# A two-layer graph network on one core: the last quad by one level of the short product, its graphs normalised alone, the first degrees planned with a longer transfer, and a new order of the work

## The chip, the core and the metric

The kernel runs on one core of a Trainium2 chip. A core has five engines with a program each: TensorE (PE, matmuls, with a separate load of the stationary operand, PEld), VectorE (DVE), ScalarE (ACT), GpSimd (POOL) and SyncE (SP, which only issues transfers here). Matmuls write to eight PSUM banks of 128 partitions by 512 numbers. The metric is the device time of one execution in microseconds (us); less is better. Everything is computed in 32-bit floating point.

## What is computed

There are 128 graphs of 128 nodes with 512 features each. `x` and `adj` are the inputs, `W`, `W1`, `W2`, `W3` the weights.

```python
def layer0(x, adj, W):
    deg = jnp.sum(adj, axis=-1, keepdims=True)
    agg = jnp.einsum('bij,bjf->bif', adj, x) / jnp.maximum(deg, 1e-6)
    return relu(jnp.einsum('bnf,of->bno', jnp.concatenate([x, agg], 2), W))

def gcn(x, adj, W, b):
    return jnp.einsum('bnm,bmh->bnh', adj, jnp.einsum('bnf,fh->bnh', x, W)) + b

def layer1(x, adj):
    x = relu(gcn(x, adj, W1, b1))
    x = relu(gcn(x, adj, W2, b2))
    return gcn(x, adj, W3, b3)

x = layernorm(x + layer0(x, adj, W))
x = layernorm(x + layer1(x, adj))
```

## The kernel before

**Quads.** Four graphs make a quad, 512 rows; there are 32 quads (`NG`). Each of the big products of a quad (512 rows by 512 features by 512 columns) is done in a short form of block multiplication: the matrices are cut in two by two blocks, sums and differences of blocks are made, and seven block products stand for eight. The products carry numbers 1 to 7, with 1 and 5 first, and results are put together from them by copies on ScalarE (L570 into an SBUF tile `s`, L576 into another bank, L636 and L806 into the result) and adds on VectorE (L325).

- With **one level**, `product` (L590) is one block product: four matmuls of 128x256.
- With **two levels**, each of the seven is cut again in the same way: `inner_product` (L608) works on 128x128 blocks, 49 matmuls of 128x128 in place of 28 of 128x256. The sums of the second level are made by `inner_sums`, for the data on GpSimd into tiles `ti`, in part over the data themselves, and for W2 and W3 once, on VectorE: they overwrite the block `b01` of each weight form by `b01 - b00`. The function `two(q)` says that W2 and W3 are multiplied by two levels for all quads but the first. The layer-0 product does so from quad 2 on, with the forms of W0 (there called "forms") kept in DRAM and streamed through `ring` and `big` tiles.

**Stages.** Each quad passes the stages X (load of the transposed x and its sums), D (adjacency and degrees), AT (transposed adjacency), L0 to L3 (layer-0 product), A0 and A1 (aggregation with the normalised adjacency, first layernorm), G0 to G3 (aggregation for layer 1, L897), Ha and Hb (product with W1), Sa and Sb (product with W2), H2 (aggregation with relu, L978 and L989), Ta and Tb (product with W3), and Z0 and Z1 (aggregation of two graphs each, L1018, residual, second layernorm, output). The products with W1 are always of one level; bias and relu follow on ScalarE (L942).

**Order.** The whole program is written out at build time. A string `ORDER` lists stages with a lag ("Tb-5" is stage Tb of the quad five behind), `AFTER` says which stages a stage has to follow, and a planner (`Plan`) takes the resulting list of operations, estimates a cost for each, works out a latest time for each, and fills the five engines' programs by a simulation of its own. Constants steer it: `HELP` (how near its latest time an add of GpSimd has to be for VectorE to take it), `HOLD` (how long a bank may stay full), `LEADS` (how much ahead of its latest time an operation may start: for the seeding of banks, a second use, the data's inner sums, and the streamed forms). Each engine then runs its program strictly in order. Only SP and, for quad 0's degrees, ScalarE issue transfers; these rotate over eight completion semaphores, and a transfer waits for the one before it on its semaphore.

**The degrees.** `degrees(q)` (L546 to L548) sums the rows of the four adjacencies, takes the larger of sum and 1e-6, and its reciprocal, `deg`. It writes these 512 numbers to DRAM (`dd`), and reads them back as one row that is repeated over all partitions (`ah`), to scale the transposed adjacency. The second transfer waits for the first. For quad 0 both are on ScalarE's queue. The planner counts the first with a size of 400,000 bytes; it moves 2 KB.

**The end.** The last quad (31) does the same as the others: two-level S and T stages with inner sums on GpSimd or VectorE, then Z0 and Z1, each with two graphs' layernorm: VectorE's statistics (L821, L822), a square root on ScalarE (L826), reciprocal and a multiply on VectorE (L829, L833), the two graphs' scaling on ScalarE (L841), and their outputs of 256 KB each by SP. By `AFTER`, Z0 and Z1 both follow Tb.

Of the kernel before, what the change touches and what calls it, by code (L numbers as in the profile page):

```python
# [14 lines left out]
P = 128  # L15
# [20 lines left out]
class Plan:  # L36
# [5 lines left out]


    LAG = 0.15
    AHEAD, HELP, HOLD, SEEN, REST, SPARE = 32, 12.0, 3.0, 8, 15.0, 1
    DMA_US, DMA_RATE = 2.0, 0.22e6

    def __init__(self, pools):
# [176 lines left out]

BANKS = 8
SIZES = 8, 3, 7, 6
LEADS = 3.8, 7.0, 45.3, 276.2
AFTER = {
    "X": "L2-1+1 L3-1+1", "D": "A0-1 A1-1 D-1", "AT": "Z0-2 Z1-2", "L0": "X D AT A1-1 A0-1 Z0-2 Z1-2", "L1": "L0", "L2": "L1", "L3": "L1 L2<2",  # L230
    "A0": "L2 L3", "A1": "L2 L3", "G0": "A0 Hb-1", "G1": "A0 Hb-1", "G2": "A1 Hb-1", "G3": "G0 G1 G2 A1",
    "Ha": "G3 Tb-1!", "Hb": "Ha", "Sa": "Hb Z0-1! Z1-1!", "Sb": "Sa", "H2": "Sb", "Ta": "H2", "Tb": "Ta", "Z0": "Tb", "Z1": "Tb",
}
ORDER = """
    Tb-5 Tb-5 AT-4 L0-4 Sa-5 D L1-4 H2-5 L1-4 L1-4 L2-4 L3-4 L2-4 L2-4 L3-4 L2-4 L1-4 H2-5 Sb-4 Z1-6 H2-5 A1-4 A1-4
    H2-5 Z1-6 G0-4 H2-5 L0-3 Z0-6 Ha-4 Sb-4 Ha-4 A0-4 L3-4 X-3 D L2-4 Sb-4 L0-3 Hb-4 Tb-5 Tb-5 G1-4 L0-3 Ta-5 G2-4
    G1-4 L2-4 Tb-5 G3-4 L2-4 L3-3 L2-4 Ta-5 Ta-5 G0-4 Ta-5 Ha-4 Ta-5 A1-4 A0-4 G3-4 Z0-5 L0-3 Ta-5 AT-3 Hb-4 L0-3 G2-4
    L1-3 Sa-4 L0-3 Sb-4 Ta-5 Sa-4 Ta-5 L3-3 Hb-4 Tb-5 Sa-4 Sb-4 Ha-4 X-2 Sb-4 Sa-4 Sa-4 L1-3 A0-3 Z1-5 Z0-5 L3-3 Sb-4
    Sb-4 L3-3 L1-3 Sa-4 Ha-3 Ha-3 Sa-4 L0-3 L1-3 Tb-4 Tb-4 L3-3
"""  # L240


# [1 line left out]
def gnn_resnorm_kernel(  # L244
# [62 lines left out]
    def pinned(ins):  # L307
        return tc.keep_in_program_order(ins)
# [11 lines left out]
    def const(v):  # L320
        return lambda: v
# [14 lines left out]
    class Weight:  # L336
# [17 lines left out]
        def inner_sums(self, over=()):  # L354
            for ps in HALVES:
# [5 lines left out]
                for dst, a, b, reads, writes in (  # L361
# [4 lines left out]
                ):  # L366
                    add("DVE", len(ps) * P, const(dst), const(a), const(b), reads, writes, OP.subtract, True)

        def to_forms(self, s):

            for ps in PAIRS:
                n = len(ps)
                t = self.t[:, ps[0] : ps[-1] + 1].rearrange("p k c (o n) -> p k c o n", o=2)
                b00, b01, b10, b11 = (t[:, :, c, o] for c in range(2) for o in range(2))
                raw = [(self.name, p) for p in ps]
                f, e = Slot("ti"), Slot("ti")

                def form(sl, j, n=n):
                    return lambda: TI_T[sl.index][:, j, 0:n]

                def send(i, src, reads, ps=ps):
                    dma(
                        const(FORMS[i - 1][:, ps[0] : ps[-1] + 1, s]), src, reads, [("form", s, i, p) for p in ps],
                        len(ps) * P * P * 4,
                    )

                def sub(dst, a, b, reads, writes, n=n):
                    add("DVE", n * P, dst, a, b, reads, writes, OP.subtract, True)

                sub(form(f, 1), const(b11), const(b01), raw, [f, e, (f, 1)])  # L390
                sub(form(f, 0), const(b01), const(b00), raw, [f, (f, 0)])
                sub(form(e, 0), const(b11), form(f, 0), raw + [f, (f, 0)], [e, (e, 0)])
                sub(form(e, 1), const(b10), form(e, 0), raw + [e, (e, 0)], [e, (e, 1)])
                send(1, const(b00), raw)
                send(2, const(b10), raw)
                send(3, const(b11), raw)
                send(7, form(f, 1), [f, (f, 1)])
                send(5, form(f, 0), [f, (f, 0)])
                send(6, form(e, 0), [e, (e, 0)])
                send(4, form(e, 1), [e, (e, 1)])  # L400
# [25 lines left out]
    class Data:  # L426
# [8 lines left out]
        def keys(self, places, cs=range(2), gs=range(2)):  # L435
            return [(self.name, p, c, g) for p in places for c in cs for g in gs]

        def sums(self):
            for d, a, b, op in ((3, 1, 5, OP.add), (2, 3, 0, OP.subtract), (1, 0, 1, OP.subtract), (6, 4, 2, OP.subtract)):
                add(  # L440
                    "POOL", F, const(self.t[:, d]), const(self.t[:, a]), const(self.t[:, b]),
                    self.keys((a, b)), self.keys((d,)), op,
                )

        def inner_sums(self):
# [96 lines left out]
    def degrees(q):  # L542
# [3 lines left out]
        vector(512, lambda: pinned(nc.vector.tensor_reduce(d, AR_T, axis=AX.X, op=OP.add)), ["ar"], kd)  # L546
        vector(90, lambda: pinned(nc.vector.tensor_scalar(d, d, DEG_EPS, None, op0=OP.max)), kd, kd, True)
        vector(90, lambda: pinned(nc.vector.reciprocal(d, d)), kd, kd)  # L548
        dma(const(dd.rearrange("g i -> i g")), const(d), kd, [("dd", q % 2)], 400000, queue)
        dma(  # L550
            const(AH_T), const(bass.AP(tensor=dd.tensor, offset=dd.offset, ap=[[0, P], [P, G], [1, P]])),
            [("dd", q % 2)], ["ah", "row of degrees"], 400000, queue,
# [258 lines left out]
    def rows_b(key, a, b, t):  # L811
        yield from wino_b(key, a, b, copy_to(t, 1, 0), sums_to(t, 0, 1))

    def layernorm(i, ap, keys):

        i %= ND
        mv, rs = MV_T[i], RS_T[i]
        for j in range(2):
            st = ST_T[(2 * i + j) % ND]
            ks = [("st", (2 * i + j) % ND)]  # L820
            vector(512, lambda j=j, st=st: pinned(nc.vector.bn_stats(st, ap(j))), keys(j), ks)  # L821
            vector(98, lambda j=j, st=st: pinned(nc.vector.bn_aggr(mv[:, j, :], st)), ks, [("mv", i, j)])  # L822
        mk = [("mv", i, 0), ("mv", i, 1)]
        kr, kb = ("rs", i, 1), ("rs", i, 2)
        scalar(
            2, lambda: pinned(nc.scalar.activation(rs[:, 0, :], mv[:, :, 1], AF.Sqrt, bias=EPS_T)), mk + ["eps"], [kr],  # L826
            columns=1,
        )
        vector(90, lambda: pinned(nc.vector.reciprocal(rs[:, 0, :], rs[:, 0, :])), [kr], [kr])  # L829
        vector(  # L830
            90,
            lambda: pinned(
                nc.vector.scalar_tensor_tensor(rs[:, 1, :], mv[:, :, 0], -1.0, rs[:, 0, :], op0=OP.mult, op1=OP.mult)  # L833
            ),
            mk + [kr], [kb], True,
        )
        for j in range(2):
            scalar(
                512,
                lambda j=j: pinned(  # L840
                    nc.scalar.activation(ap(j), ap(j), AF.Identity, bias=rs[:, 1, j : j + 1], scale=rs[:, 0, j : j + 1])  # L841
                ),
                [kr, kb] + keys(j), keys(j), columns=2,
            )

    WBA = Streamed()
# [108 lines left out]
    def seg_h1_b(q):  # L955
        d = data(q, "h1")
        yield from wino_b(("h1", q), data(q, "g1"), W1, lambda p: relu_to(d, 1, p), sums_h1(q, 0, 1), transposed=True)
        d.sums()
        if two(q):
            d.inner_sums()  # L960

    def seg_s2_a(q):
        yield from (single_a if two(q) else rows_a)(("s2", q), data(q, "h1"), W2, row(q, "s2"))

    def seg_s2_b(q):
        yield from (single_b if two(q) else rows_b)(("s2", q), data(q, "h1"), W2, row(q, "s2"))

    def seg_h2(q):
        d, s = data(q, "h2"), row(q, "s2")
        a, ka = at(q)  # L970
        for o in (2, 3, 0, 1):
# [22 lines left out]
                [p, "b2"], d.keys((4 * h, 4 * h + 1), (c,)), columns=1,  # L994
            )
            yield
        d.sums()
        if two(q):
            d.inner_sums()

    def seg_s3_a(q):
        yield from (single_a if two(q) else rows_a)(("s3", q), data(q, "h2"), W3, row(q, "s3"))

    def seg_s3_b(q):
        yield from (single_b if two(q) else rows_b)(("s3", q), data(q, "h2"), W3, row(q, "s3"))

    def seg_last(q, m):
# [3 lines left out]
        for j, o in enumerate(os):  # L1011
# [11 lines left out]
                "DVE", F, lambda o=o: S_T[o.index], lambda p=p: bank_ap(p), const(u.graph(g)),  # L1023
                [p] + u.keys((g,)), [o],
            )
            yield
        layernorm(4 * q + 2 + m, lambda j: S_T[os[j].index], lambda j: [os[j]])
        for j, o in enumerate(os):
            dma(
# [157 lines left out]
```

## Time and profile before

The median of three runs is 2274.39 us, from 2273.63 to 2274.56. The profiled execution took 2272.34 us; its span from the first to the last instruction is 2270.6 us at a mean granted TensorE clock of 0.997.

| engine | busy us | share of the span | instructions |
|---|---|---|---|
| PE | 2241.7 | 99% | 13704 |
| PEld | 1973.0 | 87% | 13704 |
| DVE | 1555.7 | 69% | 3321 |
| POOL | 1274.7 | 56% | 1673 |
| ACT | 1236.9 | 54% | 2378 |

PE's first matmul starts at 8.54 us, its last ends at 2261.18. The costliest groups of PE are the two-level products (L608), then the one-level ones (L590), then the aggregations (L872, L897, L978, L1018). Some unit times of the trace, which serve as measures: four matmuls of 128x256 take 1.73 us, one of 128x128 takes 0.2225, one of 128x512 takes 0.86; ScalarE copies 128x512 in 0.59, VectorE adds 128x512 in 0.69, GpSimd in 1.27.

How to read the rows that follow in the next section: the list of waits tells which engine and line waited for which other, for how long in total, how often and how long at most. A row of windows gives a stretch of the span, its length, each engine's busy time in it, the granted clock of PE as a share of full speed, the share of time that the transfer engines were busy, and GB/s. The chain of waits goes back from the last instruction to what released it; each row is a start, a length and what was done; "q" behind an engine's name (SPq, ACTq) is its queue issuing a transfer. A tile is named without its number.

### The profile page before, as it was taken

To read this page: it belongs to the slowest core of one execution; us is meant where nothing else is said; L and a number is where in the kernel's file an instruction comes from. 1 tells how busy PE (TensorE), PEld (TensorE's weight loads), DVE (VectorE), ACT (ScalarE), POOL (GpSimd) and SP (SyncE) were. 2 spreads that over 40 slices of the span, in tenths; PEclk is the share of its full clock that TensorE was granted. 3 is DMA by queue.
4 is the path that set the end of the run, shared out by engine and by line. 5 is a ranking of instruction groups with operands and counts; after the bars stand their busy time and mean duration, and the time that the engine had idled before them with its cause. 6 is when DMAs were issued, how large, how long until landed. Compare 5 with 4: busy or idle time off the path is not lost.

```text
span 2270.6 us, 39980 instructions
## 1 busy us (share of the span) xinstructions
PE 2241.7 (99%) x13704; PEld 1973.0 (87%) x13704; DVE 1555.7 (69%) x3321; ACT 1236.9 (54%) x2378; POOL 1274.7 (56%) x1673
## 2 busy tenths in 40 slices
PE   8999999999999999999999999999999999999997
PEld 6888888898898888888988988888888888898895
DVE  4766667766676667677666776676776667666666
ACT  2455555555555555555555555555555555555554
POOL 0236655656656566556565565665565655656641
PEclk9999999999999999999999999999999999999999
DMA  7644445534455444555344554445553445534431
GB/s 232 156 144 132 137 157 167 178 116 148 132 174 170 136 139 131 161 171 166 125 140 138 179 170 128 143 133 161 170 157 125 137 146 170 174 116 143 126 103 38
DMA packets 218330, 333.14 MB, mean 147 GB/s; under 512 B 39313, under 2 KB 83857, under 8 KB 218129
## 3 DMA queue, kind: packets, MB, share of 16 engines
q1 hardware_dynamic: 217456, 330.33, 46.1%
q8 instruction: 110, 1.80, 0.4%
q14 instruction: 92, 0.75, 0.1%
q10 hardware_dynamic: 672, 0.26, 0.0%
HBM read 290.46 MB, written 40.04 MB: 146 GB/s over the span
## 4 chain that ended last, share of the span: by engine, by line
PE 97%; DMA 1%; DVE 1%; ACT 0%; issue 0%; POOL 0%; SPq 0%; ACTq 0%; DVEq 0%
PE bank L608 58%; PE bank L590 20%; PE bank L897 5%; PE bank L978 5%; PE bank L1018 5%; PE bank L872 5%; DMA dd<-deg 0%; DMA s<-in_x_dram 0%; DMA big<-in_w0T_dram 0%; ACT s L570 0%; ACT s L841 0%; DVE st L821 0%; DVE T L325 0%; POOL ti L327 0%; DVE xT L325 0%
## 5 line engine op out<-in xcount | busy, mean ns | idle before, releaser
L570 ACT COPY s<-bank 128x384 f32<-128x384 f32 (+1 forms) x569 | 307.7, 541 | 512.7 <-PE bank L608 340.5
L590 PE MATMUL bank<-T,w 128*128 128x256 f32 x1792 | 407.2, 379 | 0.0
L590 PEld LDWEIGHTS bank<-T,w 128*128 128x128 f32 x1792 | 335.7, 190 | 43.9 <-issue 0.5
L608 PE MATMUL bank<-big,ti 128*128 128x128 f32 (+1 forms) x1712 | 329.0, 326 | 0.0
L325 DVE TENSOR_TENSOR v<-bank,s 128x512 f32<-128x512 f32 x244 | 167.4, 686 | 222.0 <-PE bank L608 193.3
L327 POOL TENSOR_TENSOR T<-T 128x512 f32<-128x512 f32 (+2 forms) x275 | 246.6, 917 | 107.1 <-PE bank L590 87.4
L608 PEld LDWEIGHTS bank<-big,ti 128*128 128x128 f32 x1712 | 262.3, 191 | 37.4 <-issue 18.2
L608 PE MATMUL bank<-ring,xT 128*128 128x256 f32 x1140 | 290.0, 380 | 0.0
L327 POOL TENSOR_TENSOR xT<-xT 128x512 f32<-128x512 f32 (+1 forms) x249 | 242.0, 972 | 72.4 <-DVE rstd L833 36.3
L576 ACT COPY bank<-bank 128x512 f32<-128x512 f32 (+2 forms) x277 | 144.9, 523 | 194.8 <-PE bank L608 133.4
L325 DVE TENSOR_TENSOR T<-T 128x512 f32<-128x512 f32 (+1 forms) x345 | 210.0, 637 | 46.2 <-ACT T L921 43.8
L608 PEld LDWEIGHTS bank<-w,ti 128*128 128x128 f32 x1736 | 221.5, 192 | 20.0 <-issue 7.6
L608 PE MATMUL bank<-w,ti 128*128 128x128 f32 x1736 | 235.1, 276 | 1.2 <-DVE row L325 0.7
L608 PEld LDWEIGHTS bank<-big,T 128*128 128x128 f32 x1680 | 215.9, 191 | 15.5 <-issue 6.7
L608 PE MATMUL bank<-w,T 128*128 128x128 f32 x1680 | 228.1, 276 | 0.0
L608 PE MATMUL bank<-big,T 128*128 128x128 f32 x1680 | 223.9, 276 | 2.9
L327 POOL TENSOR_TENSOR s<-s,v 128x384 f32<-128x384 f32 (+1 forms) x62 | 70.1, 1130 | 278.5 <-ACT bank L692 170.0
L608 PEld LDWEIGHTS bank<-w,T 128*128 128x128 f32 x1680 | 215.9, 192 | 11.9 <-ACT bank L576 5.7
L327 POOL TENSOR_TENSOR v<-v 128x384 f32<-128x384 f32 (+2 forms) x90 | 88.8, 1002 | 231.8 <-DVE u L325 127.2
L608 PEld LDWEIGHTS bank<-ring,xT 128*128 128x128 f32 x1140 | 201.3, 191 | 19.1
L325 DVE TENSOR_TENSOR row<-bank,s 128x384 f32<-128x384 f32 (+2 forms) x252 | 117.0, 464 | 119.2 <-PE bank L608 79.7
L325 DVE TENSOR_TENSOR v<-v 128x512 f32<-128x512 f32 (+1 forms) x278 | 184.4, 672 | 9.0 <-DVE v L325 0.5
(85 smaller groups left out, 3957.1 us busy)
## 6 DMA issues: line engine op xcount, KB each, us to landing
ring<-forms SPq DMA_DIRECT2D x339, 256.0 KB, 3.0
big<-forms SPq DMA_DIRECT2D x291, 256.0 KB, 4.4
s<-in_x_dram SPq DMA_DIRECT2D x128, 256.0 KB, 5.1
out_dram<-s SPq DMA_DIRECT2D x128, 256.0 KB, 5.3
xT<-in_xT_dram SPq DMA_DIRECT2D x62, 512.0 KB, 7.1
big<-forms SPq DMA_DIRECT2D x110, 128.0 KB, 2.0
ring<-forms SPq DMA_DIRECT2D x100, 128.0 KB, 2.2
ar<-in_adj_dram SPq DMA_DIRECT2D x32, 256.0 KB, 2.9
```

What stands on the lines that cost most here:

```text
L325: on_vector = lambda: pinned(nc.vector.tensor_tensor(dst(), a(), b(), op=op))
L327: on_gpsimd = lambda: pinned(nc.gpsimd.tensor_tensor(dst(), a(), b(), op=op))
L570: scalar(n * P, lambda: pinned(nc.scalar.copy(quarters_of(s, n), quarters(p, n))), [p], [s])
L576: scalar(n * P, lambda: pinned(nc.scalar.copy(quarters(s, n), quarters(p, n))), [p], [s])
L590: nc.tensor.matmul(bank_ap(p)[:, o, :], lhsT, rhs, start=start and o == 0 and c == 0, stop=c == 1, skip_group_check=True,)
L608: nc.tensor.matmul(dst, ta(), tb(), start=start and n == 0, stop=True, skip_group_check=True)
L872: nc.tensor.matmul(bank_ap(p), AH_T[:, g, :], y.graph(g), start=False, stop=True, skip_group_check=True)
L897: nc.tensor.matmul(bank_ap(p)[:, c // 2, (c % 2) * P : (c % 2 + 1) * P], u.chunk(g, c), a[:, g, :], start=c == 0, stop=True, skip_group_ch ...
L978: nc.tensor.matmul(bank_ap(p)[:, g // 2, (g % 2) * P : (g % 2 + 1) * P], s.chunk(g, o), a[:, g, :], start=g == 0, stop=True, skip_group_ch ...
L1018: nc.tensor.matmul(bank_ap(p), a[:, g, :], s.graph(g), start=False, stop=True, skip_group_check=True)
```

## The change

1. **The last quad by one level.** H1's and H2's outer sums go to VectorE; no inner sums are made; W2 and W3 are put back to their first-level form by `restore()` (b01 gets b00 added again); S2 goes by `columns_a` and `columns_b`, S3 by `rows_at_end_a` and `rows_at_end_b`, which take the products in another order. S3's makes the rows of graphs 0 and 1 first.
2. **Z0 of the last quad** may go after Ta (`AFTER`).
3. **The last two graphs are normalised one by one** (`layernorm` with `js`), the scaling of each is split in half between ScalarE and VectorE (`halves`), and their outputs leave in four transfers of 128 KB.
4. **The planner** counts quad 0's `dd` with 1,600,000 bytes; `HELP`, `HOLD` and `LEADS` have other values; `ORDER` is another string.

```diff
-    AHEAD, HELP, HOLD, SEEN, REST, SPARE = 32, 12.0, 3.0, 8, 15.0, 1
+    AHEAD, HELP, HOLD, SEEN, REST, SPARE = 32, 16.0, 5.0, 8, 15.0, 1
...
-LEADS = 3.8, 7.0, 45.3, 276.2
+LEADS = 6.9, 7.0, 29.0, 448.5
...
-    "Ha": "G3 Tb-1!", "Hb": "Ha", "Sa": "Hb Z0-1! Z1-1!", "Sb": "Sa", "H2": "Sb", "Ta": "H2", "Tb": "Ta", "Z0": "Tb", "Z1": "Tb",
+    "Ha": "G3 Tb-1!", "Hb": "Ha", "Sa": "Hb Z0-1! Z1-1!", "Sb": "Sa", "H2": "Sb", "Ta": "H2", "Tb": "Ta", "Z0": "Ta Tb!", "Z1": "Tb",
...
-    Tb-5 Tb-5 AT-4 L0-4 Sa-5 D L1-4 H2-5 L1-4 L1-4 L2-4 L3-4 L2-4 L2-4 L3-4 L2-4 L1-4 H2-5 Sb-4 Z1-6 H2-5 A1-4 A1-4
...
+    L3-4 L0-4 Ta-6 H2-5 L3-4 Tb-5 Sa-5 L1-4 L1-4 Hb-5 D Tb-6 L2-4 L3-4 G0-4 Z0-6 Sb-4 D L2-4 L2-4 Tb-5 L0-3 L0-3 L1-4
...
+        def restore(self):
+            for ps in HALVES:
+                t = self.t[:, ps[0] : ps[-1] + 1].rearrange("p k c (o n) -> p k c o n", o=2)
+                raw = [(self.name, p) for p in ps]
+                add("DVE", len(ps) * P, const(t[:, :, 0, 1]), const(t[:, :, 0, 1]), const(t[:, :, 0, 0]), raw, raw, OP.add, True)
...
-                    "POOL", F, const(self.t[:, d]), const(self.t[:, a]), const(self.t[:, b]),
-                    self.keys((a, b)), self.keys((d,)), op,
+                    "DVE" if at_end else "POOL", F, const(self.t[:, d]), const(self.t[:, a]), const(self.t[:, b]),
+                    self.keys((a, b)), self.keys((d,)), op, at_end,
...
-        dma(const(dd.rearrange("g i -> i g")), const(d), kd, [("dd", q % 2)], 400000, queue)
+        dma(const(dd.rearrange("g i -> i g")), const(d), kd, [("dd", q % 2)], 400000 if q else 1600000, queue)
...
-    def layernorm(i, ap, keys):
+    def layernorm(i, ap, keys, js=(0, 1), halves=None):
...
+            if halves is not None:
+                k0, k1 = halves
+                scalar(
+                    256, lambda: pinned(nc.scalar.activation(ap(j)[:, 0], ap(j)[:, 0], AF.Identity, bias=b, scale=r)),
+                    kr + kb + keys(j), k0, columns=2,
+                )
+                vector(
+                    256, lambda: pinned(nc.vector.tensor_scalar(ap(j)[:, 1], ap(j)[:, 1], r, b, op0=OP.mult, op1=OP.add)),
+                    kr + kb + keys(j), k1, True,
+                )
+                continue
...
-        d.sums()
-        if two(q):
+        d.sums(at_end=q == NG - 1)
+        if two(q) and q < NG - 1:
             d.inner_sums()
...
     def seg_s2_a(q):
+        if q == NG - 1:
+            W2.restore()
+            yield from columns_a(("s2", q), data(q, "h1"), W2, row(q, "s2"))
+            return
...
+    def columns_a(key, a, b, t):
+        px, py, pz = Slot("bank"), Slot("bank"), Slot("bank")
+        product(px, a, b, 2, True, False)
+        yield
+        product(py, a, b, 1, True, False)
+        s1 = copied(py)
+        sums_to(t, 0, 0)(s1, px)
+        yield
+        product(py, a, b, 6, False, False)
+        s2 = copied(py)
+        yield
+        product(pz, a, b, 5, True, False)
+        yield
+        product(py, a, b, 7, False, False)
+        s3 = copied(py)
+        sums_to(t, 1, 1)(s3, pz)
...
+    def columns_b(key, a, b, t):
+        product(pz, a, b, 3, False, False)
+        sums_to(t, 0, 1)(s2, pz)
+        yield
+        product(py, a, b, 4, False, False)
+        copy_to(t, 1, 0)(py)
...
+    def rows_at_end_a(key, a, b, t):
+        product(px, a, b, 2, True, False)
+        yield
+        product(py, a, b, 1, True, False)
+        s1 = copied(py)
+        sums_to(t, 0, 0)(s1, px)
+        yield
+        product(pz, a, b, 5, True, False)
+        s5 = copied(pz)
+        yield
+        product(py, a, b, 6, False, False)
+        s2 = copied(py)
+        yield
+        product(pz, a, b, 3, False, False)
+        sums_to(t, 0, 1)(s2, pz)
...
+    def rows_at_end_b(key, a, b, t):
+        product(py, a, b, 7, False, False)
+        sums_to(t, 1, 1)(s5, py)
+        yield
+        product(py, a, b, 4, False, False)
+        copy_to(t, 1, 0)(py)
...
     def seg_s3_a(q):
+        if q == NG - 1:
+            W3.restore()
+            yield from rows_at_end_a(("s3", q), data(q, "h2"), W3, row(q, "s3"))
+            return
...
+            if q == NG - 1 and m == 1:
+                ks = [(o, h) for h in range(2)]
+                layernorm(4 * q + 3, lambda j: S_T[os[j].index], lambda j: [os[j]], (j,), [[k] for k in ks])
+                for h in range(2):
+                    dma(
+                        const(out[q][:, g, h * H : (h + 1) * H]), lambda o=o, h=h: S_T[o.index][:, h],
+                        [o, ks[h]], [("out", q, m, j, h)], P * H * 4,
+                    )
             yield
+        if q == NG - 1 and m == 1:
+            return
```

In the built programs PE has 6854 matmuls before and 6812 after: 98 of 128x128 go, 56 of 128x256 come. VectorE has 3323 instructions before and 3554 after, GpSimd 1678 and 1405. At the start of the changed program the adjacency load of quad 0 stands ninth on SP's queue, ahead of four loads of W0 that it followed before, and its reduction stands twelfth on VectorE instead of twentieth; on ScalarE the write of `dd` is the third operation on data instead of the sixth, and the read-back of `ah` has one more copy ahead of it.

## The prediction, made before the changed kernel was run

> **What bounds the kernel now.** I read the busy table first, then TensorE's waits, then three stretches of the span (start, middle, end), then the chain of waits inside the start and the end.
>
> The first tells that TensorE (PE) is the bound: 2241.7 of 2270.6 us. The waits say how little of the rest any other engine could give in the middle:
>
> ```profile
> PE bank L590 <- DMA big<-in_w0T_dram: 5.4, 1, 5.4
> PE bank L590 <- ACT s L570: 3.0, 1, 3.0
> PE bank L608 <- DVE xT L325: 2.8, 1, 2.8
> PE bank L608 <- ACT s L570: 2.5, 4, 0.7
> ```
>
> The columns are: who waits, for whom, total us, times, longest. Each wait stands at the start or in the last quad. The windows (busy us and count by engine, then the granted clock) agree:
>
> ```profile
> 30.00:36.00 6.00, 5.48 (x13) 4.41 (x14) 0.99 (x2) 1.54 (x3) 0.00 (x0) 0.50 0.87 262
> ...
> 600.00:1200.00 600.00, 599.23 (x3702) 529.20 (x3702) 415.11 (x882) 334.19 (x646) 361.02 (x475) 1.00 0.47 148
> ...
> 2240.00:2247.00 7.00, 6.28 (x37) 5.90 (x38) 4.46 (x15) 1.98 (x4) 0.46 (x1) 0.76 0.01 1
> ```
>
> In the middle PE works 599.23 of 600 us; only fewer matmuls could shorten it. At the start and the end the clock falls to a half after a gap. So the change is priced in three places: start, steady part, end.
>
> **The start.** Chain of waits, start and length in us:
>
> ```profile
> 19.09 0.18 DVE deg L548
> 19.27 0.02 issue
> 19.29 10.07 DMA dd<-deg
> 29.36 0.02 issue
> 29.38 0.02 ACTq L318
> 29.40 0.04 issue
> 29.44 0.35 ACTq L318
> ```
>
> The write of quad 0's inverse degrees (2 KB, one 4-byte element at a time) takes 10.07 us. ScalarE's queue then stands before the read-back (ah), and the copy of PE's last bank stands behind it, 29.88 to 30.47. PE's product ends at 27.51, the next starts at 30.52, and granted clock 0.50 follows. The first aggregation matmul (L872) starts at 40.48. Between 27.51 and 40.48 stand four products, 4 x 1.73 = 6.92 (the rate of 1.73 per product is that of full clock), so 6.05 us are lost: 3.0 of gap, some 3.05 of half clock.
>
> In the changed program the adjacency load stands ahead of four W0 loads, the reduction comes right behind quad 0's data sums on VectorE, and the write is ScalarE's third operation instead of its sixth. Before, the reduction ran at 16.74 and the reciprocal ended at 19.27; now I get about 14.4 for the reciprocal, hence issue at about 14.5, landing at 24.6 (10.07, as here) to 26.5 (12.0, the longest of the 32 writes). The copy that PE lacked now stands ahead of the read-back: the 3.0 us gap goes, and the half clock with it.
>
> But the read-back is not free yet. DMAs rotate over eight completion semaphores, and an issue waits for the previous DMA on its own. The read-back now shares one with the eighth store of W0 forms (128 KB, SP's DMA 28); the third of these stores shares the degree write's. So SP stands still until the write has landed, then issues six stores at 0.45 to 0.5 each, and the sixth lands some 2 us later: landing + 4.7. That puts the read-back at 29.3 to 31.2, central 30.0, hardly earlier than 29.44. What is behind it on ScalarE: two copies (0.35 + 0.59 + 0.59 + 0.04 = 1.57 later), on which the third of the four products waits. That could start at 27.51 + 3.46 = 30.97; with 31.57 it waits 0.6, say 0.7 (0 to 1.9). First aggregation 27.51 + 6.92 + 0.7 = 35.1. The read-back itself, landing 3.5 after issue (29.44 to 32.96 before) plus 0.68 of multiply, is there at 34.2. **Start: -5.4** (-6.0 to -4.2).
>
> The rule and the row differ here. The Trainium skill, "TensorE: Matmul & The Clock Gate", section on HAM oscillation, wants no PE-idle gap over about 3.4 us. Gaps of 3.0 (start) and 2.82 (end) are under that, so by the rule no clock is lost and removing them is worth 3.0 + 2.8 alone. By the rows clock 0.50 follows both, and no gap of 0.81 or less has it. I take the rows: 3.05 more here, 1.7 more at the end. A new 1.9 us gap lies between; the trace doesn't show which side, and half clock there would cost another 3.
>
> **The fill, 35 to 135 us.** PE is without a gap from 36 on, so 5.4 us gained must also be fed 5.4 us earlier. On SP's queue the degree writes of quads 1 to 3 now stand ahead of quad 1's four x loads. Here a DMA behind such a write on a shared semaphore went out only after it landed (62.65 to 74.63 the write, 74.92 the next forms load). Counted from the products that release them, the x loads land some 10.5 us after; layer 1 of quad 1 can then start about 0.7 later than PE would. Bounds: 0 (PE takes other quads' work) and 4 (one write lands late and PE runs dry). Nearest row is the 0.7: **+1.**
>
> **The steady part.** About 8 of GpSimd's adds of 128x256 per quad go to VectorE (1678 to 1405 and 3323 to 3554 instructions in all). VectorE takes 0.42 where GpSimd took 0.73: +3.3 us in a quad of 69.6, so VectorE goes from 69% to some 73%, GpSimd from 56% to some 49%. They lie beside PE. PE's own order differs by a few swapped products per quad, its instructions are the same, and SP's order around the degree write is nearly line for line that of before, with the write and the read-back at the same places. Two longer leads let seeds of banks and streamed weights go earlier, as buffers allow. **0**; below nothing it can't go by more than the 2.9 us PE idles between 100 and 2200; if cover goes it is the rival below.
>
> **The end.** From the end of the last H1 product (2216.19) to PE's end (2261.18) are 44.99 us. The work: Z of quad 30 and 31, 8 x 0.86 = 6.9; H2's 16 x 0.2225 = 3.56; S2 and S3 by two levels, 2 x 49 x 0.2225 = 21.8; together 32.2. So 12.8 are lost: eight gaps of 7.3, half clock from 2241.5 to 2244.9 costing 1.7, and 3.7 of restarts after gaps. The longest gap:
>
> ```profile
> 2236.13 0.70 ACT xT L989
> 2236.82 0.02 issue
> 2236.85 0.43 DVE ti L325
> 2237.28 0.02 issue
> 2237.31 0.42 DVE ti L325
> 2237.73 0.64 DVE xT L325
> ```
>
> Three more sums follow, until 2239.92; PE has nothing else in hand. They are the inner sums (and outer sums) of the second level, which the change drops for this quad.
>
> Added: S2 and S3 are then 28 matmuls of 128x256 each, 28 x 0.432 = 12.1 instead of 10.9: **+2.4**. The restored weights are four VectorE adds (0.69 and 0.46 twice), done while PE works on the quad before; they'd cost PE only if later than the first S2 and S3 product, and 2 to 3 us of cover are there. Going through the new order product by product, with copies of 0.59, adds of 0.69 and relus of 0.47 between, every product finds its input but one: the last two Z matmuls wait 0.66 for the copy of the last S3 product. Z of graphs 0 and 1 now stands between S3's last two products. So 32.2 + 2.4 + 0.7 = 35.3. **-9.7**. Bounds: -10.4 with no wait, -7 with four unforeseen ones of 0.66 (the size of the gaps of before).
>
> After PE's end:
>
> ```profile
> 2264.33 0.80 ACT s L841
> 2265.13 0.70 ACTq L1182
> 2265.84 1.41 ACT s L841 x2
> ```
>
> Four graphs' normalisations end at 2267.25, outputs issue to 2267.27, land at 2269.56, the span ends 9.42 after PE. Now two graphs alone remain: add to +0.71, statistics to +1.9, root and reciprocal to +2.8, half a graph each on ScalarE and VectorE to +3.7. SP issues four half outputs, the last at +4.55; 128 KB land about 2.0 later (stores of that size: 1.63 to 2.3), then 1.04 as before: +7.6. **-1.8.** The Trainium skill, "DMA: Bandwidth & Descriptors", Rules for kernel authors, speaks against this: join many small transfers into one, since small ones pay mostly a fixed price. By the row the fixed price is there (256 KB 2.27, 128 KB about 2.0), but they overlap; whole graphs would be normalised at +4.4, issued and landed at +6.7, halves land at +6.55. Splitting is worth 0.2 by the rows, and two extra issues of 0.45, 0.9 lost, if the fixed price ruled: -1.1. I take -1.8; it is the pairing alone that carries it.
>
> **Sum:** -5.4 + 1 + 0 - 9.7 - 1.8 = -15.9, from the profiled execution's 2272.34 to 2256.4 (span 2270.6 to 2254.7). The median of the runs shown, 2274.39, is 2.05 above the profiled one, so 2258.5.
>
> **Rivals.**
> - *A recurring stall (slower).* The degree write occupies SP's queue 8 to 12 us in each quad, and x and forms loads stand behind. If the new order has PE wait once per quad, or VectorE at 73% delivers one sum late, it costs s in each of some 29 quads. It decides from 16.9 / 29 = 0.58 us per quad; one wait of 0.7 (PE's usual gap) gives 2274.39 - 16.9 + 20.3 = 2277.8 (16.9 is the gain without the fill's 1 us). For: slack at the tightest banks is tenths of a us. Against: PE's and SP's orders are nearly the old ones, and GpSimd is relieved.
> - *The start gives little.* The write lands at 26.5, the third product waits 1.9 and the half clock returns (3), and the fill takes 4: the start gives 1.2; 2258.5 + 4.2 + 3 = 2265.7. For: the shared semaphore. Against: the 10.07 measured.
> - *The end keeps waits.* Two-level gaps go, but one-level products come in a chain, and each needs ScalarE between normalisations: four waits of 0.66 leave -7.0, so 2261.2. For: the eight gaps of before are of this kind. Against: the order walked through above has one.
> - *Longer time planned for the write does nothing.* It moves orders, not the transfer: the read-back is issued where it was (30.0 against 29.44). I expect this in part; the gain is in what stands ahead of it.
>
> **Chances.** Forecast 0.64, start rival 0.15, end rival 0.14, recurring stall 0.07. Under 0.2% (4.5 us) the measurement tells no change: between 2269.9 and 2278.9. Faster takes the first three less a little: 0.90; the stall is split around its breakeven: same 0.04, slower 0.06. Range: from 2252.5 (start 0.6 better, no loss in the fill, the end's wait gone 0.7, the 2.9 of the middle, 0.8 behind PE's end) to 2267 (start rival with a bit).
>
> **What would show it.** First aggregation at 35.1, no clock of 0.50 before 40 and after 2220; read-back issued near 30; 600 to 1200 at 599 busy; from H1's last product to PE's end 36 to 37 with Tb's last 1.3 in it; 7.6 from there to the span's end. Wrong if a wait of PE appears in every quad, if x loads of quad 1 stall PE near 70 to 110, or if S2 waits for restored weights.

## The result, and the profile after

The median went from 2273.89 us (2272.26 to 2274.56, six runs) to 2261.83 us (2261.17 to 2263.64, six runs): -12.1 us, ratio 0.9948 with a 95% interval of 0.9935 to 0.9961. The forecast was 2258.5 in a range of 2252.5 to 2267. The profiled executions are 2272.34 and 2261.35 us, their spans 2270.6 and 2259.4: -11.2, where the sum of the prediction said -15.9. (The start of 8.54 us given above for PE's first matmul is that of the last matmul of the first product; the first starts at 5.42, in both kernels.)

PE's waits after; the columns are as in the list of before:

```profile
PE bank L596 <- DMA big<-in_w0T_dram: 5.4, 1, 5.4
PE bank L914 <- ACT u L859: 2.0, 1, 2.0
PE bank L614 <- DMA big<-forms: 1.1, 1, 1.1
PE bank L596 <- DVE T L325: 0.8, 1, 0.8
PE bank L1109 <- ACT row L812: 0.7, 1, 0.7
```

The 3.0 us of the start and the eight waits of the last quad are gone; the one of 0.7 that is left there is the one that the sum had. The second and third rows are new, and both lie in the fill. Windows of the same execution (length, busy us and count by engine, granted clock, share and rate of transfers):

```profile
30.00:36.00 6.00, 6.00 (x30) 5.28 (x29) 1.60 (x3) 3.01 (x6) 0.00 (x0) 1.00 0.97 250
100.00:112.00 12.00, 8.89 (x45) 7.30 (x45) 8.81 (x22) 3.76 (x8) 1.16 (x2) 1.00 0.91 268
600.00:1200.00 600.00, 599.23 (x3700) 528.60 (x3699) 443.51 (x964) 335.81 (x645) 313.51 (x394) 1.00 0.48 148
```

From 30 to 36 PE is busy without a gap at clock 1.00 (5.48 of 6.00 at 0.50 before). The middle is the same to the hundredth, 599.23, with VectorE at 443.51 in place of 415.11. Most of what was gained at the start is lost at 100 to 112: 3.1 us without a matmul. The end (rows of "issue" under 0.05 us are left out here and in the chains below):

```profile
2235.11 10.36 PE bank L596 x48
2245.47 1.72 PE bank L1109 x4
2247.18 1.74 PE bank L596 x8
2248.95 0.59 ACT row L812
2249.59 2.00 PE bank L1109 x4
2251.61 0.69 DVE s L325
```

S3's first six products follow each other without a wait, then Z of graphs 0 and 1, the last product, the one copy that PE waits for, and Z of graphs 2 and 3. The span ends 7.8 us after PE.

Added up by place, from the starts of the matmuls in the two traces (time between two matmuls less that matmul's usual pitch):

| place | predicted | profiled execution |
|---|---|---|
| to the first aggregation | -5.4 | -4.3 (40.48 to 36.16) |
| fill, from there to 175 | +1.0 | +3.9 |
| steady part, 175 to 2190 | 0 | +0.1 |
| last quad to PE's end, 2.4 of work added | -9.7 | -9.3 |
| from PE's end to the span's end | -1.8 | -1.6 |
| sum | -15.9 | -11.2 |

### The profile page after: what moved, and what is told of

It reads as the page before. It is cut to its first block, busy times and chain, and to the rows that moved or that the text cites. A ratio compares the mean times of both kernels' runs of the same rounds, so it can differ in the third digit from the quotient of the medians.

```text
span 2259.4 us, 39677 instructions
## 1 busy us (share of the span) xinstructions
PE 2238.6 (99%) x13620; PEld 1967.4 (87%) x13620; DVE 1632.7 (72%) x3552; ACT 1237.8 (55%) x2369; POOL 1112.0 (49%) x1400
## 4 chain that ended last, share of the span: by engine, by line
PE 98%; DMA 1%; DVE 0%; issue 0%; ACT 0%; SPq 0%; ACTq 0%; DVEq 0%
PE bank L614 58%; PE bank L596 21%; PE bank L914 5%; PE bank L1002 5%; PE bank L1109 5%; PE bank L889 5%; DMA s<-in_x_dram 1%; DMA big<-in_w0T_dram 0%; DVE st L828 0%; DVE u L896 0%; DVE big L325 0%; SPq L318 0%; ACTq L1283 0%; ACT u L859 0%; ACT T L1013 0%
## 5 line engine op out<-in xcount | busy, mean ns | idle before, releaser
L327 POOL TENSOR_TENSOR xT<-xT 128x512 f32<-128x512 f32 (+1 forms) x244 | 236.6, 970 | 137.6 <-DVE ah L325 41.4
L327 POOL TENSOR_TENSOR T<-T 128x512 f32<-128x512 f32 (+2 forms) x250 | 253.0, 1028 | 69.5 <-ACT T L925 38.1
L614 PE MATMUL bank<-big,ti 128*128 128x128 f32 (+1 forms) x1410 | 261.7, 317 | 0.0
L614 PE MATMUL bank<-big,xT 128*128 128x256 f32 x976 | 253.9, 380 | 1.1 <-DMA big<-forms 1.1
L614 PEld LDWEIGHTS bank<-w,ti 128*128 128x128 f32 x1680 | 215.9, 192 | 18.9 <-issue 7.2
L614 PE MATMUL bank<-w,ti 128*128 128x128 f32 x1680 | 226.5, 275 | 0.0
L614 PEld LDWEIGHTS bank<-w,T 128*128 128x128 f32 x1680 | 213.6, 192 | 10.4 <-ACT bank L582 5.7
L614 PEld LDWEIGHTS bank<-big,ti 128*128 128x128 f32 x1410 | 204.6, 191 | 18.6 <-issue 4.8
L327 POOL TENSOR_TENSOR s<-s,v 128x512 f32<-128x512 f32 (+1 forms) x60 | 68.1, 1135 | 282.1 <-DVE T L325 165.3
L614 PEld LDWEIGHTS bank<-big,xT 128*128 128x128 f32 x976 | 174.7, 190 | 19.6 <-DMA big<-forms 1.7
L325 DVE TENSOR_TENSOR v<-v 128x512 f32<-128x512 f32 (+1 forms) x270 | 179.1, 672 | 8.5 <-DVE v L325 0.5
```

What stands on the lines that cost most here:

```text
L325: on_vector = lambda: pinned(nc.vector.tensor_tensor(dst(), a(), b(), op=op))
L327: on_gpsimd = lambda: pinned(nc.gpsimd.tensor_tensor(dst(), a(), b(), op=op))
L614: nc.tensor.matmul(dst, ta(), tb(), start=start and n == 0, stop=True, skip_group_check=True)
```

## Experiments

Each run has four or five times of its own and seven or eight of the kernel before beside it; with so few the interval of a ratio is some 0.15% (3.4 us) to either side, and a profile shows a single execution. So times decide where the distance is large, and the profile where it is small.

### What holds the fill up

The chain of waits of the changed kernel there:

```profile
91.75 0.02 SPq L318
91.80 12.58 DMA s<-in_x_dram
```

A load of quad 1's x takes 12.58 us; the page's median for such loads is 5.1. (Landings here and below are read from the steps of the transfers' semaphores.) On SP's queue the degree write of quad 3 went out at 90.79, the four loads at 91.25 to 92.71. The write landed at 102.06, the loads at 102.22 to 106.02, one behind the other.

**One write on another queue.** Engines other than SP and ScalarE keep their programs.

```diff
-    dma(..., [("dd", q % 2)], 400000 if q else 1600000, queue)
+    dma(..., [("dd", q % 2)], 400000 if q else 1600000, "ACT" if q == 3 else queue)
```

> The changed kernel with one transfer moved: the degree write of quad 3, which stands on SP's queue directly ahead of quad 1's four x loads (issued 90.79, x loads issued 91.25 to 92.71, landing 102.2 to 106.0), goes to ScalarE's queue instead. Every other engine keeps its program. Theory A (transfers issued behind a degree write on the same queue land only after it): the x loads land 4 to 6 us after issue, the two waits of PE at 105.2 and 108.3 (1.1 and 2.0, with restart and pitch 3.6) go, about 2258.2 against 2261.8. Rival B (PE is simply too early in the fill and the transfers are at their rate): the x loads land late all the same and the waits stay within 1 us of 3.1: 2261 to 2262. Rival C (a degree write slows every transfer in flight, whatever the queue): x loads land some 10 us after issue, waits as now.

The loads took 3.6 to 5.6 us and both waits are gone (0.55 of loss from 100 to 175 in place of 4.11), so B falls. But this run can't tell A from C. SP had stood 2.5 us before the write, for the degrees; without it the four loads go out at 88.79 to 90.17, ahead of the write, which ScalarE issues at 91.69 and which lands at 105.74. What SP issues behind it in time lands late all the same, though on another queue. The three `ring` loads of 92.42 to 95.10 land at 104.19 to 105.94; the rows give the median time to landing, in this run and in the next one, where the writes are short (there the third load falls outside the window of the row):

```profile
ring<-forms SPq DMA_DIRECT2D x3, 256.0 KB, 11.1
ring<-forms SPq DMA_DIRECT2D x2, 256.0 KB, 6.7
```

The kernel before has the same on one queue, and also for transfers issued ahead of the write. From 59.54 to 60.24 stores take 3.8 to 4.4 us; the last store and the adjacency load ahead of the write of 62.65 (issued at 61.69 and 62.14) take 11.1 and 10.9, and the two stores behind it (63.96, 64.47) 11.0 and 10.6. The last two numbers of a window are share and rate of transfers; the first row is of the kernel before, the second of this run:

```profile
65.00:72.00 7.00, 7.00 (x41) 6.36 (x40) 4.94 (x9) 3.30 (x7) 0.00 (x0) 1.00 1.10 58
101.00:107.00 6.00, 6.00 (x29) 5.31 (x28) 3.43 (x14) 1.93 (x5) 0.70 (x2) 1.00 0.76 31
```

In the run with short writes it is 289 GB/s from 93 to 102. So C is nearer: while such a long write is on its way, most transfers in flight come to a near stop, on its queue and on the other one. What helped here is that the loads were ahead of it by 1.5 to 2.9 us and had landed by 95.78; that the queue by itself matters is not shown. The time is 2262.26 (2259.6 to 2263.6), no better, though 2258.2 was expected; in the profiled execution other waits came that cost 3.6 us together, four of them these:

```profile
PE bank L596 <- ACT bank L582: 2.5, 4, 0.7
```

They are taken up in the last section.

**A short write.** The same numbers in 128 pieces of 16 bytes; the order in DRAM is another, so the aggregation of layer 0 is scaled by other nodes' degrees.

```diff
-    dma(const(dd.rearrange("g i -> i g")), const(d), ...
+    dma(const(bass.AP(tensor=dd.tensor, offset=dd.offset, ap=[[G, P], [1, G]])), const(d), ...
```

> The changed kernel with every degree write made in 128 pieces of 16 bytes in place of 512 of 4 bytes; the 512 numbers then stand in another order in DRAM, so the aggregation of layer 0 is scaled by other nodes' degrees. Same program order. Theory A (the number of pieces makes the 10 us, and what is behind them on the queue waits): a write lands in 3 to 4 us, quad 1's x loads land some 5 us after issue, the waits in the fill go (-3.6), the start has no wait to lose; about 2258. Rival B (transfers at their rate): waits in the fill stay, 2261 to 2262. If the 10 us are not set by the number of pieces, the write takes 8 to 10 us still and nothing changes.

2255.89 (2255.7 to 2258.27), ratio 0.9919 (0.9904 to 0.9934). The writes land in 1.4 us in the quickest and 5.8 in the slowest case, where they took 7.9 to 12.0 in the changed kernel. No wait is left in the fill. So the number of pieces makes the long time, as theory A of this run has it. The fill is 3.6 of the 5.9 us by which the time is under the changed kernel; what the rest is, these runs don't show.

**The planned size as before.** `1600000` becomes `400000` for quad 0.

> The changed kernel with the planner counting quad 0's degree write as before (400,000). The start's order is then that of before up to the first aggregation, and on SP the degree write of quad 3 falls behind quad 1's x loads. Theory A: the start loses its 6.0 again (first aggregation at 40.5 instead of 36.2, or 34.3 at full clock), the fill has no wait (-3.6 to -3.9): net +0.4 to +2.4, 2262 to 2264.5. Rival (the waits in the fill come from the new order string, not from this size): start lost and waits kept, some 2266 to 2268.

2266.53 (2265.16 to 2267.29). The start is that of before, with 4.2 us of wait and half clock (first aggregation at 41.52), and the fill has no loss (0.19); quad 3's write goes out at 114.26 there, long after quad 1's loads (94.28 to 95.66). So the planner's size is what moves the write at the start and, through the order that follows, what puts quad 3's write ahead of quad 1's loads: it takes with one hand and gives with the other. The time is 2 above the expected range; the profile has four of the waits just named (2.3 us).

### The last quad alone, and the order alone

**The last quad's part in the kernel before.** String, constants and size of before; all engines' programs are those of before until the last two quads.

> The kernel before with the last quad's part alone (one level, rows first, graphs normalised alone, Z0 after Ta), the order string, the planner's constants and the degree write's size as before; the programs of all engines are those of before until the last two quads. Theory: the end alone carries the gain, 9.3 from the last H1 product to PE's end and 1.6 behind it, so 2263.2 (10.9 under 2274.1), and start and fill are those of before (first aggregation 40.5, no wait of PE in 100 to 175). Rival: the end's program runs without waits only because the new order was made for it; then PE keeps 3 or more waits after 2200 and the time is 2265 to 2270.

2264.04 (2260.98 to 2265.35), ratio 0.9952 (0.9937 to 0.9967): 10.4 of the 12.1 us, as the theory has it. Beside the wait of 0.7 that the changed kernel has too, two of 0.7 were left, at 2187 and 2198.

**The order alone.** String, constants and size of after, the last quad of before.

> The changed kernel with the last quad's part taken out: new order string, new constants, degree write counted as 1,600,000 for quad 0, last quad as before. Theory: what the start gains (4.3, or 6.2 where full clock is there from the first gap on) the fill gives back (3.6 to 3.9), the steady part gives nothing or loses up to 2 to delays at the degree writes: 2271.5 to 2274.5. Rival: the new order brings several us that the last quad's part only hides: 2267 or less.

2284.08 (2281.97 to 2286.97), ratio 1.0043 (1.0029 to 1.0057): **slower than before by 9.6.** Neither theory had this. The start is that of after, the fill loses 6.4, two waits of 1.1 in the steady part are of the kind told in the last section, and the last quad of before loses 18.9 from 2150 on in place of 13.2. Some of PE's waits:

```profile
PE bank L608 <- ACT bank L692: 3.5, 2, 2.0
...
PE bank L897 <- ACT u L841: 2.1, 1, 2.1
PE bank L608 <- DMA big<-forms: 2.0, 1, 2.0
```

The first row is seeds of the two-level products, which the changed last quad doesn't have; behind the longer of the two the clock falls to 0.50 for 6.83 us, from 2263.26 on. The other two are the waits of the fill, longer than in the changed kernel, and 3.41 us at 0.50 follow them too. The two parts don't add up: -10.4 and +9.6 alone, -12.1 together.

**The new string with constants of before.** The text on record says that the order string was that of before. It was not: the kernel that ran had the new string, and only `HELP`, `HOLD`, `LEADS` and the planned size of before.

> The kernel before with the last quad's part alone (one level, rows first, graphs normalised alone, Z0 after Ta); order string, planner constants and the degree write's size as before. Theory: the end alone carries the gain, -9.3 in the last quad and -1.6 behind PE's end, so 2263.0 (10.9 under 2273.9). If the new order string is needed for the last quad's program to run without waits, the end keeps some of its gaps and the time is 2265 to 2269.

2305.38 (2300.74 to 2307.01), so it says nothing on the last quad, but much on the string: 31 above before. This is the first rival of the prediction, a wait that recurs. Two runs tell which constants: the old `LEADS` alone, and the old `HELP` and `HOLD` alone.

> The changed kernel with the leads of before (3.8, 7, 45.3, 276.2), all else as changed. With the new string and all the constants of before PE had two waits in each quad (VectorE's sums of T 0.8, a streamed form 1.1) and the time was 2305. Theory (streamed forms that may go out 276 instead of 448 ahead, and inner sums begun earlier, make these waits): both waits in some 15 to 29 quads, 2280 to 2305. Rival (HELP and HOLD make them): no recurring wait, 2260 to 2265.

> The changed kernel with HELP 12 and HOLD 3 as before (how near its latest time an add has to be for VectorE to take it from GpSimd, and how long a bank may stay full), leads and size as changed. With the new string and all the old constants PE had two waits in every second quad and 2305; with the old leads alone it had none. Theory: these two constants make the waits: 0.8 for VectorE's sums of T and 1.1 for a streamed form, each 10 to 15 times, 2280 to 2305. Rival (they come only where leads and these two are old together): no recurring wait, 2260 to 2266.

2262.59 (2262.1 to 2263.3) and 2303.01 (2301.29 to 2304.25). My theory for the leads was wrong; it is HELP and HOLD. PE's waits in the last of these runs:

```profile
PE bank L614 <- DVE T L325: 13.2, 16, 0.8
PE bank L614 <- DMA big<-forms: 11.8, 15, 1.9
...
PE bank L914 <- ACT u L859: 3.0, 1, 3.0
```

Some 16 waits of 0.8 for a sum on VectorE and 15 for a streamed form, and the middle stretch falls from 599.23 to 592.32 busy us of 600. Which of the two constants it is wasn't tried.

### The parts of the end

**Two graphs as a pair, two transfers of 256 KB.** `if q == NG - 1 and m == 1` is made false in both places.

> The changed kernel with the last two graphs normalised as a pair and put out as two transfers of 256 KB, as before. Theory: from PE's end to the span's end 8.5 to 9 in place of 7.8: statistics of both graphs, then one root, then two whole scalings one behind the other on ScalarE (0.8 each, the second 1.5 after the first), +0.9 (+0.5 to +1.5): 2262.7. Rival (small transfers pay mostly a fixed price, so four cost more than two): no change or a gain, 2261.5 or less.

The time, 2264.57 (2263.67 to 2267.0), holds three of the extra waits (2.2 us) and can't tell. The end can: PE ends at 2254.82 and the span at 2262.6, 7.7 later, as good as in the changed kernel (7.8). The chain:

```profile
2257.32 0.18 DVE rstd L836
2257.52 0.17 DVE rstd L840
2257.72 0.81 ACT s L859
2258.53 0.70 ACTq L1283
```

The last whole graph goes out at 2259.31 and lands 2.25 later; the last half went out at 2256.22 and landed 2.03 later. From PE's end that is 6.7 and 6.7: what a half gains in scaling it loses in two more issues. The rule that the prediction drew on (the Trainium skill, "DMA: Bandwidth & Descriptors", Rules for kernel authors) says of transfers under 64 KB that they pay mostly overhead. These are larger, and a fixed part still rules: 128 KB take 1.91 to 2.03, 256 KB 2.25. The expected +0.9 was wrong, the 0.2 of the prediction nearer.

**The usual order of products.** `columns_a/b` and `rows_at_end_a/b` become `rows_a/b`.

> The changed kernel with the last quad's S2 and S3 by one level but in the order of products that the other one-level stages have (1, 5, 6, 2, 7, 4, 3); all else as changed. Theory (dropping the second level and its inner sums makes the gain of the end, the order of the products little of it): from the end of the last product of Tb of quad 30 to PE's end 36 to 38 in place of 35.6, and up to 0.8 more behind PE's end since the rows of graphs 0 and 1 are not first: time +0.5 to +3. Rival (the order makes most of it): 4 or more waits of 0.5 to 0.8 in the last quad, some 39.5 or more.

2262.69 (2261.99 to 2262.99). From the end of Tb's last product to PE's end 35.6 us, as changed (35.6), with one wait of 0.7 at another place. But behind PE's end it is 9.5 in place of 7.8: four graphs are finished there again:

```profile
2250.85 1.34 DVE s L325 x2
2252.19 1.19 DVE st L828 x2
2253.38 0.28 DVE mv L829 x3
2253.66 0.58 DVE st L828
```

So the 9.3 come from dropping the second level and its sums, and the 1.6 behind PE need the order of the products that makes the rows of graphs 0 and 1 first. Which part Z0's earlier place has in them wasn't tried by itself.

### A version that beats both

Here the degrees stay node by node, so that the short write is right: the read-back is a contiguous row, and the multiply and the aggregation's stationary operand read with a stride of four numbers.

```diff
-    AH_T = tile_of([P, G, P], "ah")
+    AH_T = tile_of([P, P, G], "ah")
+    AH_V = AH_T.rearrange("p n g -> p g n")
...
-            const(AH_T), const(bass.AP(tensor=dd.tensor, offset=dd.offset, ap=[[0, P], [P, G], [1, P]])),
+            const(AH_T), const(bass.AP(tensor=dd.tensor, offset=dd.offset, ap=[[0, P], [G, P], [1, G]])),
...
-        add("DVE", 512, const(AH_T), const(t), const(AH_T), k + ["ah"], ["ah"], OP.mult, True)
+        add("DVE", 512, const(AH_V), const(t), const(AH_V), k + ["ah"], ["ah"], OP.mult, True)
```

It was put into the changed kernel, and into the kernel before with the last quad's part (old string, old constants).

> The changed kernel with the degree numbers kept node by node: each write is 128 pieces of 16 bytes, the read-back is one contiguous row, and the multiply and the stationary operand of layer 0's aggregation read with a stride of four numbers; the result is the reference's. Theory: as the run with the short write, 2256 (2255.5 to 2258.5), no wait of PE between 20 and 2200. Rival: strided weight loads or the strided multiply cost more than they do now (0.19 and 0.68): 32 quads x 4 loads at twice the time would show as +0.19 x 128 = up to 24 us.

> The kernel before with the last quad's part and with the degrees kept node by node (short write, contiguous read-back, strided multiply and weight loads); order string, constants and planned sizes as before. Theory (what the new order gains at the start is only the hiding of the slow write): the write lands 2 to 3 us after 19.3, the read-back goes out before 24, PE has no wait and no clock of 0.50 between 20 and 45; against the run with the last quad's part alone (2264.0) the start gives 6.0 and the delays at the writes up to 2: 2257.5 (2255.5 to 2258.5), as good as the changed kernel with the same degrees (2258.6). Rival (the new order is worth several us of its own): 2261 or more.

2258.59 (2258.26 to 2259.03), ratio 0.9930 (0.9915 to 0.9945), and 2258.49 (2257.44 to 2259.99), ratio 0.9937 (0.9922 to 0.9952). Both beat the changed kernel's 2261.83, with ranges of times that don't meet (their intervals overlap its own). The first is just above its expected range of 2255.5 to 2258.5, the second at its edge. PE's waits with the new order:

```profile
PE bank L597 <- DMA big<-in_w0T_dram: 5.5, 1, 5.5
PE bank L597 <- DVE T L326: 0.8, 1, 0.8
PE bank L1110 <- ACT row L813: 0.7, 1, 0.7
```

And the start with the old order:

```profile
21.14 0.34 ACTq L319 DMA_DIRECT2D dd<-deg  x1
22.50 0.58 ACT L813 COPY row<-bank 128x512 f32<-128x512 f32 x1 [1.14 <-PE bank L597]
23.78 0.35 ACTq L319 DMA_DIRECT2D ah<-dd  x1
27.73 0.58 ACT L577 COPY s<-bank 128x512 f32<-128x512 f32 x1 [4.65 <-DMA forms<-big]
```

The write lands 2.56 after its issue, the read-back goes at 23.78, and ScalarE's next copy is in time: PE has no wait from 20 to 45. With a short write these runs show no gain of the searched order (2258.6 against 2258.5, each to some 3.4 us; spans of the profiles 2256.8 and 2257.5). At the start it had been a way around the 10 us. The strided reads are slower and hidden: weight loads 310 ns in place of 190 beside matmuls of 594, the multiply 1.11 us in place of 0.68.

## Why the prediction was right, and where it was off

- **The end** was right in mechanism and size: 35.6 from Tb's last product to PE's end (35.3 predicted), with the one wait of 0.7 where it was put. The gap for inner sums went, and the half clock behind it with it, as the rows had it, and not the 3.4 us of the Trainium skill ("TensorE: Matmul & The Clock Gate", section on HAM oscillation).
- **Behind PE's end** 7.8 against 7.6. The split that was weighed there is worth nothing; the gain is that only two graphs are left.
- **The start** was right step by step: write issued at 15.71 (14.5 predicted), landed at 24.93 (24.6 to 26.5), read-back issued at 30.27 (30.0), no half clock. So the rival "longer planned time does nothing" holds for the read-back and not for the time. The first aggregation came at 36.16, not 35.1, since the clock became full 3.6 us later than in the profile of before: see the last section.
- **The fill is the step that was mis-sized**: "+1", where PE lost 3.9, near the upper bound of 4 that the text had. One of its own signs of being wrong came true: x loads of quad 1 stalled PE, at 110.69, and the forms loads behind them at 106.70. The x loads landed 13.5 after the product that was to release them, not 10.5 (90.88 to 104.38 for the second): the write ahead of them took 11.27, and they landed one after another behind it. The row had been misread. In the kernel before, the forms transfer of "74.92" did not go out after the write had landed at 74.63: it went out at 63.96, on another semaphore, and landed at 74.92. So the shared semaphore was not what held it, and a transfer issued just behind a write had to be priced at the write's own length and its place in the line.
- **The steady part** is 0 in the profile, and the rival of a recurring stall did not come true; but the runs with old HELP and HOLD show how near it was: 28 to 31 us slower than before with the same string. That the searched constants avoid it is in no row of before, so this 0 was in part luck. So was the clock in the fill: the gap of 2.0 us cost no clock, and a gap of the same size in the order alone did (see the last section).

## What to carry over

A transfer of many tiny pieces costs most to the transfers in flight with it. Before an order is searched around it, shorten it: with 128 pieces of 16 bytes in place of 512 of 4 the old order, with the new last quad, was as fast as the new one, as far as these runs can tell. A searched order holds only with the constants and the stages it was searched for; with the last quad of before the new order was 10 us slower than the old one, and with the old HELP and HOLD 28 to 31 us slower than the whole kernel before, so parts of such a change can't be priced by adding them up.

## What the runs showed of the hardware

**The clock at the start differs from run to run.** The first product's matmuls start every 0.427 us, later ones every 0.216. The short step comes from 10.30 on in the profile of before and from 13.93 in that of the changed kernel; the trace's first record of the granted clock stands at 9.22 and 13.82, and the windows show 1.00 ahead of it only for want of a record. The time lost before 20 us is 2.9 in the profiles of before and of the planned size of before, and 4.6 to 5.4 in the twelve others. The old start came both ways (2.9 twice, 4.6 to 4.7 three times), so 1.7 us of this are no property of the program; all nine profiles with the new start are late, and whether it can come early isn't shown. In the changed kernel it makes PE 1.9 us later than in the profile of before, and hides the wait of 0.7 that the prediction had: the third product starts at 32.71, its copy ended at 31.81; 1.9 earlier it would have waited some 1.0 (an estimate from these times).

**The clock goes by stretches of 3.41 us, not by the length of one gap.** In all 14 traces the records of the granted clock begin on a grid of 3.413 us that lies differently in each (before: 9.22, 29.70, 36.52, so six and two stretches). I added up PE's idle time in each stretch at full clock. Nine had 2.07 to 3.24 us of it, and clock 0.50 followed each; all others had at most 1.93, and it followed none. At half clock, nine stretches had at most 0.10 idle and full clock followed; three had 0.72 to 1.95 and it stayed at half. So it counts where a gap falls. The gap of 2.00 us before 110.69 in the changed kernel lies in two stretches, 0.70 and 1.30; one of 2.07 before 111.70 in the order alone lies in one. What follows, changed kernel first:

```profile
110.70:116.00 5.30, 5.30 (x40) 5.09 (x41) 3.78 (x10) 5.13 (x9) 2.13 (x3) 1.00 0.34 85
112.90:116.20 3.30, 3.30 (x17) 3.30 (x16) 2.58 (x8) 1.92 (x5) 1.45 (x3) 0.50 0.12 14
```

This is a fit to these traces; no run moved a gap to test it.

**Around the landing of degree writes of 4-byte pieces, other engines' signals come late now and then.** In the profiles with one write on ScalarE's queue, with the planned size of before, and with paired outputs, 12 waits of 0.5 to 1.1 us came in the steady part. From the first:

```profile
1158.81 1.73 PE bank L596 x8
1160.54 1.58 PE bank L614 x10
1162.12 0.58 ACT bank L582
```

The product ends at 1160.54, but ScalarE's copy of it starts at 1162.12, and it had nothing else to do. In the trace PE's semaphore counts of 1160 to 1162 arrive together at 1162.04, 1162.12 and 1162.17; the degree write issued at 1150.38 lands at 1162.06. All 12 waits end 11.7 to 12.4 us after the issue of such a write, and PE has no other wait of more than 0.1 us in the steady part of these three. Five more of this kind (11.4 to 12.3 us after the issue) stand in the profiles of the order alone, of the new string with constants of before, and of the old HELP and HOLD. None is in the three profiles with short writes, but none in five others with long ones either, those of before and of the changed kernel among them. That the long write causes them is likely by its place in time, and wasn't tested by itself.
